# Seven stores for two batch tiles instead of eight, the fifth across the end of a tile

## The chip, the cores and the metric

The kernel runs on one core of one Trainium2 chip. The metric is the time on the device in microseconds (us), the median of several executions. A ratio between two kernels is the mean time of one kernel's runs over that of the other's runs of the same rounds, so it isn't quite the ratio of the medians that are quoted.

## The reference

For every batch row and every pair of fields i < j of 32 fields with 64 values each, the vector of field i goes through the pair's own 64 x 64 matrix, and the result is multiplied element by element with the vector of field j.

```python
vi = inputs[:, i_idx, :]              # (4096, 496, 64), pairs i < j
vj = inputs[:, j_idx, :]
vdotw = jnp.einsum('bpd,pde->bpe', vi, W)
inter = vdotw * vj
return inter.reshape(B, -1)           # (4096, 31744) float32
```

520 MB are written, 42 MB are read. There are 32 batch tiles of 128 rows.

## The kernel before

TensorE multiplies into PSUM, VectorE (DVE) multiplies PSUM by the fields and writes into a ring in SBUF, and SyncE issues the stores from the ring to memory. "Unit" below means 64 columns: 64 float32 numbers, 256 B, in each of 128 rows. The work goes by two neighbouring fields at a time: step p (0 to 15) of a tile, "the pair of fields p" below, makes all products of the fields 2p and 2p + 1 with the later ones. That is 61 - 4p units, a tile 496. The ring has 440 units. A store is issued when all of its units are made, and a store that doesn't fit behind the last one begins again at 0. A product that writes to a place of the ring must wait until every earlier store from that place has landed.

```python
STORES = [[0, 1], [2, 3], [4, 5, 6], [7, 8, 9, 10, 11, 12, 13, 14, 15]]
RING = 28160
# ...
for t in range(NT):
    xt = slot[t]
    # ... input loads, two tiles each, from the ACT queue
    for s, group in enumerate(STORES):
        if at + store_w[s] > RING:
            at = 0
        osb = ring[:, at : at + store_w[s]]
        at += store_w[s]
        o0 = off[2 * group[0]]
        for p in group:
            # ... transposes of the input, matmuls into PSUM,
            #     DVE products into osb
        nc.sync.dma_start(
            out=out[:, t * cols + o0 : t * cols + o0 + store_w[s]], in_=osb
        )
```

Of the kernel before, what the change touches and what calls it, by code (L numbers as in the profile page):

```python
# [1 line left out]

# [6 lines left out]

F32 = mybir.dt.float32  # L10
ALU = mybir.AluOpType

P = 128
BANK = 512
BANKS = 8

STORES = [[0, 1], [2, 3], [4, 5, 6], [7, 8, 9, 10, 11, 12, 13, 14, 15]]

LOADS = [[0], [1], [2, 3], [4, 5, 6], [7, 8, 9, 10, 11, 12, 13, 14, 15]]


FIRST_HALF_AT, SECOND_HALF_AT = 9, 3
RING = 28160


def x_slots(NT):


    loads = [[(0, 0)]]
    for t in range(1, NT, 2):  # L30
        if t + 1 == NT:
            loads.append([(t, 1)])
        elif loads[-1][-1] == (t - 1, 2):
            loads.append([(t + 1, 0), (t, 1)])
        else:
            loads.append([(t, 1), (t + 1, 2)])
    return loads


@with_exitstack  # L40
def pair_bilinear_kernel(
    ctx: ExitStack,
    tc: tile.TileContext,
    x: bass.AP,
    w: bass.AP,
    out: bass.AP,
    F: int,
    D: int,
):
























    nc = tc.nc
    NT = out.shape[1] * 2 // (F * (F - 1) * D)
    NPR = F // 2

    width = [(F - 1 - i) * D for i in range(F)]
    off = [sum(width[:i]) for i in range(F)]
    cols = sum(width)  # L80


    woff = [i % 2 * D + sum(width[i % 2 : i : 2]) for i in range(F)]
    store_w = [sum(width[2 * p] + width[2 * p + 1] for p in g) for g in STORES]

    const = ctx.enter_context(tc.tile_pool(name="const", bufs=1))
    psum = ctx.enter_context(tc.tile_pool(name="ps", bufs=1, space=bass.MemoryType.PSUM))

    ident = const.tile([P, P], F32, tag="ident", name="ident")
    make_identity(nc, ident)  # L90

    def runs(tl, a, b, n):

        ap = tl[:, a : a + n]
        return bass.AP(ap.tensor, ap.offset, [list(ap.ap[0]), [b - a, 2], list(ap.ap[1])])

    xbuf = const.tile([P, 3 * F * D], F32, tag="x", name="x")
    x_loads = x_slots(NT)
    slot = {t: xbuf[:, ts(s, F * D)] for load in x_loads for t, s in load}

    def load_x(load):

        at = sum(len(before) for before in x_loads[: x_loads.index(load)]) * P * F * D
        n = len(load) * F * D
        s = load[0][1]
        nc.scalar.dma_start(
            out=xbuf[:, s * F * D : s * F * D + n],
            in_=x[at : at + P * n].rearrange("(p c) -> p c", p=P),
        )

    pring = psum.tile([P, BANKS * BANK], F32, tag="pring", name="pring")
    bank = 0

    def take_banks(n):

        nonlocal bank
        if bank + n > BANKS:
            bank = 0
        got = pring[:, bank * BANK : (bank + n) * BANK]
        bank = (bank + n) % BANKS  # L120
        return got

    xT = const.tile([P, NPR * P], F32, tag="xT", name="xT")

    def transpose_x(xt, g):

        n = 2 * BANK // P
        pt = take_banks(2)
        for c in range(n):
            nc.tensor.transpose(pt[:, ts(c, P)], xt[:, ts(n * g + c, P)], ident)  # L130
        nc.scalar.copy(xT[:, ts(g, 2 * BANK)], pt)  # L131

    ring = const.tile([P, RING], F32, tag="ring", name="ring")
    at = 0

    load_x(x_loads[0])
    w_sb = const.tile([P, sum(width[0::2])], F32, tag="w", name="w")
    done = 0
    for g in LOADS:

        upto = woff[2 * g[-1]] + width[2 * g[-1]]
        nc.sync.dma_start(out=w_sb[:, done:upto], in_=w[:, done:upto])
        done = upto

    transpose_x(slot[0], 0)
    for t in range(NT):
        xt = slot[t]
        for load in x_loads:
            if min(load)[0] == t + 1:
                load_x(load)  # L150
        for s, group in enumerate(STORES):
            if at + store_w[s] > RING:
                at = 0
            osb = ring[:, at : at + store_w[s]]
            at += store_w[s]
            o0 = off[2 * group[0]]
            for p in group:
                if p == SECOND_HALF_AT:
                    transpose_x(xt, 1)
                if p == FIRST_HALF_AT and t + 1 < NT:  # L160
                    transpose_x(slot[t + 1], 0)
                first = (width[2 * p] - 1) % BANK + 1
                for c1 in range(first, width[2 * p] + 1, BANK):
                    n = first if c1 == first else BANK
                    c0 = c1 - n
                    odd = width[2 * p + 1] and c1 > D
                    pm = take_banks(2)
                    for h in range(1 + bool(odd)):
                        a = woff[2 * p + h] + c0 - h * D
                        nc.tensor.matmul(  # L170
                            pm[:, h * BANK : h * BANK + n],
                            xT[h * D : (h + 1) * D, ts(p, P)],
                            w_sb[h * D : (h + 1) * D, a : a + n],
                            start=True,
                            stop=True,
                        )
                    xj = xt[:, (2 * p + 1) * D + c0 : (2 * p + 1) * D + c1]
                    o = [off[2 * p + h] - o0 + c0 - h * D for h in range(2)]
                    if odd and (c0 or c1 < width[2 * p]):
                        nc.vector.tensor_tensor(  # L180
                            runs(osb, o[0], o[1], n),
                            runs(pm, 0, BANK, n),
                            bass.AP(xj.tensor, xj.offset, [xj.ap[0], [0, 2], xj.ap[1]]),
                            ALU.mult,
                        )
                    else:
                        for h in range(1 + bool(odd)):
                            nc.vector.tensor_tensor(  # L188
                                osb[:, o[h] + h * D : o[h] + n],
                                pm[:, h * (BANK + D) : h * BANK + n],  # L190
                                xj[:, h * D :],
                                ALU.mult,
                            )
            nc.sync.dma_start(
                out=out[:, t * cols + o0 : t * cols + o0 + store_w[s]], in_=osb
            )


# [30 lines left out]
```

## Time and profile before

| | before |
|---|---|
| median | 1336.87 us (6 runs, 1336.71 to 1337.26) |
| DMA engines | 98.9% of the span, 422 GB/s |
| DVE | 1183.4 us busy, 89% |
| stores | 128, of 118, 102, 123, 153 units a tile |

The prediction below reckons from 1337.05 us, one of these six runs.

How to read it: the share of the DMA queues says that sixteen DMA engines work nearly all the time, so the kernel ends when the bytes are moved. One row of the groups by shape is kept here (its columns: busy us, mean ns of one, then the idle time before):

```profile
L180 DVE TENSOR_TENSOR ring<-pring,x 128x1024 f32<-128x1024 f32 x768 | 902.7, 1217 | 16.6 <-PE pring L170 4.2 <-DMA out_dram<-ring 1.5
```

### The profile page before, as it was taken

The page shows a single profiled execution, that of the slowest core. Times are in us where ns is not written, and L with a number is a line of the kernel's source. Part 1 is how long each engine was busy: PE and PEld are TensorE (multiplying, and loading weights), DVE is VectorE, ACT ScalarE, POOL GpSimd, SP SyncE. Part 2 cuts the span into 40 slices and gives each one's busy share as a digit, 9 for nine tenths or more (in the row PEclk, how much of TensorE's full clock was granted, in tenths as well). Part 3 has the DMA queues.
Part 4 walks back from the last instruction along what each step waited for, and adds up shares of the span by engine and source line. Part 5 has one row for each costly group of instructions (what it writes and reads, how often), then busy time and mean ns, then how long its engine had stood idle before and what let it go on. Part 6 is the DMA issues. An engine that isn't in the chain of part 4 may idle for free.

```text
span 1335.1 us, 13080 instructions
## 1 busy us (share of the span) xinstructions
PE 1160.6 (87%) x5376; PEld 544.9 (41%) x5376; DVE 1183.4 (89%) x1376; ACT 66.1 (5%) x65; POOL 0.7 (0%) x6
## 2 busy tenths in 40 slices
PE   6998989989899898998989889798998979989893
PEld 3443334443344443444444444344443434354441
DVE  5998989989899898998989899898998989989894
ACT  0000000000000000000000000000000000000000
POOL 0000000000000000000000000000000000000000
PEclk9999999989899999998989999899999999989997
DMA  9999999999999999999999999999999999999998
GB/s 397 433 430 430 431 428 430 418 433 430 413 425 410 436 414 427 426 414 433 405 432 431 419 429 411 432 426 421 428 413 430 426 407 417 429 421 423 429 425 352
DMA packets 21659, 562.87 MB, mean 422 GB/s; under 512 B 2400, under 2 KB 2400, under 8 KB 2656
## 3 DMA queue, kind: packets, MB, share of 16 engines
q1 hardware_dynamic: 19152, 528.49, 92.8%
q10 hardware_dynamic: 2448, 33.56, 5.9%
q8 instruction: 42, 0.69, 0.2%
q14 instruction: 17, 0.14, 0.0%
HBM read 41.94 MB, written 520.09 MB: 421 GB/s over the span
## 4 chain that ended last, share of the span: by engine, by line
DMA 47%; DVE 38%; issue 9%; PE 5%; DVEq 0%; ACT 0%
DMA out_dram<-ring 46%; DVE ring L180 32%; DVE ring L188 5%; PE pring L170 5%; DMA x<-in_x_dram 1%; DVEq L180 0%; PE pring L130 0%; ACT xT L131 0%; DVEq L225 0%; DVEq L188 0%
## 5 line engine op out<-in xcount | busy, mean ns | idle before, releaser
L170 PE MATMUL pring<-w,xT 64*128 64x512 f32 (+4 forms) x4864 | 1098.4, 564 | 146.4 <-DVE ring L180 133.5
L180 DVE TENSOR_TENSOR ring<-pring,x 128x1024 f32<-128x1024 f32 (+3 forms) x1056 | 1104.1, 1108 | 131.4 <-DMA out_dram<-ring 102.6
L170 PEld LDWEIGHTS pring<-w,xT 64*128 64x128 f32 x4864 | 489.3, 191 | 711.7 <-DVE ring L180 533.0
L131 ACT COPY xT<-pring 128x1024 f32<-128x1024 f32 x64 | 64.8, 1012 | 1224.1 <-PE pring L130 1224.1
L188 DVE TENSOR_TENSOR ring<-pring,x 128x64 f32<-128x64 f32 (+3 forms) x320 | 97.7, 356 | 2.6 <-DMA out_dram<-ring 1.9
L130 PEld LDWEIGHTS pring<-ident,x 128*128 128x128 f32 x512 | 55.6, 142 | 58.8 <-DVE ring L180 50.2
L130 PE MATMUL pring<-ident,x 128*128 128x128 f32 x512 | 70.8, 282 | 8.6 <-DMA x<-in_x_dram 8.6
L131 ACT ACT_TABLE_LOAD x1 | 1.3, 1283 | 1.7 <-PEq L221 1.7
masks.py:199 POOL TENSOR_SCALAR_AFFINE_SELECT ident<-ident 128x128 f32<-128x128 f32 x1 | 0.3, 292 | 0.1
masks.py:197 POOL MEMSET ident<- 128x128 f32 x1 | 0.2, 204 | 0.3 <-POOLq L221 0.3
L221 POOL MEMSET const-bfloat16-1.0<- 128x1 bf16 x1 | 0.1, 101 | 0.0
L221 POOL MEMSET const-uint8-127<- 128x1 uint8 x1 | 0.1, 101 | 0.0
L221 POOL MEMSET const-float32-0.0<- 128x1 f32 x1 | 0.1, 98 | 0.2 <-issue 0.2
L221 POOL MEMSET const-float32-1.0<- 128x1 f32 x1 | 0.1, 98 | 0.0
## 6 DMA issues: line engine op xcount, KB each, us to landing
out_dram<-ring SPq DMA_DIRECT2D x32, 4896.0 KB, 17.7
out_dram<-ring SPq DMA_DIRECT2D x32, 3936.0 KB, 18.1
out_dram<-ring SPq DMA_DIRECT2D x32, 3776.0 KB, 18.3
out_dram<-ring SPq DMA_DIRECT2D x32, 3264.0 KB, 18.6
x<-in_x_dram ACTq DMA_DIRECT2D x15, 2048.0 KB, 20.4
w<-in_w_dram SPq DMA_DIRECT2D x1, 2592.0 KB, 28.1
x<-in_x_dram ACTq DMA_DIRECT2D x2, 1024.0 KB, 12.8
w<-in_w_dram SPq DMA_DIRECT2D x1, 2016.0 KB, 22.2
```

The lines of the kernel that those rows point to most:

```text
L130: nc.tensor.transpose(pt[:, ts(c, P)], xt[:, ts(n * g + c, P)], ident)
L131: nc.scalar.copy(xT[:, ts(g, 2 * BANK)], pt)
L170: nc.tensor.matmul(pm[:, h * BANK : h * BANK + n], xT[h * D : (h + 1) * D, ts(p, P)], w_sb[h * D : (h + 1) * D, a : a + n], start=True, st ...
L180: nc.vector.tensor_tensor(runs(osb, o[0], o[1], n), runs(pm, 0, BANK, n), bass.AP(xj.tensor, xj.offset, [xj.ap[0], [0, 2], xj.ap[1]]), ALU ...
L188: nc.vector.tensor_tensor(osb[:, o[h] + h * D : o[h] + n], pm[:, h * (BANK + D) : h * BANK + n], xj[:, h * D :], ALU.mult,)
L221: nc = bacc.Bacc("TRN2", target_bir_lowering=False, num_devices=1)
```

## The change

The intent: fewer and larger stores, and cuts that fill the ring better. The stores are now counted over two tiles; the fifth takes the last three pairs of fields of one tile and the first three of the next.

```diff
-STORES = [[0, 1], [2, 3], [4, 5, 6], [7, 8, 9, 10, 11, 12, 13, 14, 15]]
+STORES = [0, 2, 5, 9, 13, 19, 23]
...
+    pair_at = [u // NPR * cols + off[u % NPR * 2] for u in range(NT * NPR)] + [NT * cols]
+    starts = [2 * NPR * k + u for k in range(NT // 2) for u in STORES] + [NT * NPR]
...
-        for s, group in enumerate(STORES):
-            if at + store_w[s] > RING:
-                at = 0
-            osb = ring[:, at : at + store_w[s]]
-            at += store_w[s]
...
+        for p in range(NPR):
+            u = t * NPR + p
+            if u in starts:
+                o0 = pair_at[u]
+                end = starts[starts.index(u) + 1]
+                size = pair_at[end] - o0
+                if at + size > RING:
+                    at = 0
+                osb = ring[:, at : at + size]
+                at += size
...                       # matmuls and products as before
-            nc.sync.dma_start(
-                out=out[:, t * cols + o0 : t * cols + o0 + store_w[s]], in_=osb
-            )
+            if u + 1 == end:
+                nc.sync.dma_start(out=out[:, o0 : o0 + size], in_=osb)
```

The stores are then of 118, 147, 140, 76, 186, 172 and 153 units.

## The prediction

> **What bounds the kernel now.** I read the page from the busy line to the slices, the DMA queues and the chain of waits; then the waits by engine, the groups by shape, and the chain in order of time for two tiles in mid-run.
>
> The page, with the median of 1337.05 us beside it:
>
> ```profile
> PE 1160.6 (87%) x5376; PEld 544.9 (41%) x5376; DVE 1183.4 (89%) x1376; ACT 66.1 (5%) x65; POOL 0.7 (0%) x6
> DMA  9999999999999999999999999999999999999998
> ...
> q1 hardware_dynamic: 19152, 528.49, 92.8%
> q10 hardware_dynamic: 2448, 33.56, 5.9%
> q8 instruction: 42, 0.69, 0.2%
> ...
> DMA 47%; DVE 38%; issue 9%; PE 5%; DVEq 0%; ACT 0%
> ```
>
> The queues' shares add to 98.9% of sixteen engines' span: the DMA engines are the bound, VectorE comes second at 89%. The chain alternates between DMA and DVE because each wait for ring space is followed by the work that fills the next store. That reading makes DVE look like half of the bound; it isn't, as long as the DMA queue never empties while DVE works.
>
> Who waits for a store's landing, and how seldom:
>
> ```profile
> DVE ring L180 <- DMA out_dram<-ring: 102.6, 44, 6.2
> DVE ring L180 <- PE pring L170: 17.9, 9, 13.5
> ```
>
> The figures are us in total, times and the longest. DVE stands 103 us, 2.3 us at a time, for ring space; PE costs it almost nothing after the start.
>
> The chain in order of time, between two stores of the last nine pairs of a tile:
>
> ```profile
> 582.09 21.96 DMA out_dram<-ring
> 604.05 0.03 issue
> 604.10 0.04 issue
> 604.14 1.15 DVE ring L180 x2
> ...
> 625.43 17.16 DMA out_dram<-ring
> 642.59 0.03 issue
> ```
>
> The store of 153 field widths (unit below: one width of 64 columns, 256 B a row) is issued at 582.09 and landed at 604.05, and DVE resumes 0.09 us later. Its packets themselves take 8 x 1.451 = 11.6 us on each of sixteen engines (trace: 39168 B rows, median 1451 ns, eight rows an engine), so about 4.7 us of the 17.16 were older work in the queue, 0.45 were the gap between the last packet and the last completion mark; the 21.96 also holds an input load (16384 B rows, 8 x 0.611 = 4.9 us).
>
> **One engine is late.** In the trace each store leaves sixteen completion marks. In mid-run fifteen come within about 1.5 us, and the last one 3.7 to 4.7 us behind most of them; the run's last packets end at 1329.9 to 1331.2 us on fifteen engines and at 1333.7 on one. When a 153 store is issued most engines have just run dry (first packet 0.83 us after issue; 27 such gaps, 12 us of mean engine time altogether), but the late engine still has 4.1 to 5.5 us queued. So before, the late engine never idles after the start, and the gaps of the others cost nothing. Its pace: two tiles take 81.9 us (mean of the issues from 91.19 to 1237.94, 14 pairs of tiles), less 4.9 for the input load, over 992 units: 77.6 ns a unit. The other engines need 8 x 1119 ns / 118 = 75.9.
>
> DVE's own pace, start to start without waits, added per store from the trace: pairs 0-1 8.5 us, 2-3 7.4, 4-6 9.1, 7-15 12.2; 37.1 us a tile of 496 units, or 75 ns a unit, against 41 us of DMA a tile. DVE is 10% faster than the late engine with its input load, but hardly 4% faster than its stores alone.
>
> **What the Trainium skill says.** (1) "DMA: Bandwidth & Descriptors", "Why a DMA increments its semaphore by 16 and not by 1": engines finish independently and only the full count means that all data landed. The trace agrees: sixteen marks a store, and DVE goes by the last. (2) The same page, "Specifications", gives about 27 GiB/s an engine and a 435 GB/s ceiling. The trace has 26.98 to 27.01 GB/s an engine for all four row sizes, 432 for sixteen: stores are at the ceiling, so larger ones can't be faster. (3) Same page, "Rules for kernel authors": at least 1 MiB a DMA, and coalesce small ones. All stores already have 3264 to 4896 KB, so this rule promises nothing here. (4) "Runtime: NRT & Kernel Launch", "Instruction fetch mechanics": instructions come by DMA in 16 KiB blocks of 256. The trace has 42 packets of 16384 B on the instruction queue, and 10752 PE instructions are 42 x 256. That such packets make one engine late is likely; no view proves it, and they don't change.
>
> **The change part by part.** Arithmetic, matmuls, DVE operations (1376) and their order stay. Only where a store begins and ends, and where it lies in the ring, changes. Units of the stores: before 118, 102, 123, 153 each tile; after 118, 147, 140, 76, 186, 172, 153 for two tiles.
>
> Removed: 16 stores of 128. On an engine each costs a completion mark (9 ns) and eight packet starts; from 968 ns at 26112 B and 1451 ns at 39168 B the start costs about 2 ns. 16 x (9 + 8 x 2) ns = 0.4 us. SyncE issues (0.33 us each) are off the path. So -0.4.
>
> Moved, ring: 28160 columns are 440 units, a store that doesn't fit starts again at 0. Before, the passes use 343, 373, 394, 378 units (mean 372); after 405, 434, 418, 402, 325 (mean 397). This is the gain the change is after: more data in flight at most places. But it is a gain only where it lets the late engine work, and that one has no gap to give back.
>
> Moved, granularity: nothing of a store can leave until all of it is made. 186 units are 13.7 us of DVE and 172 are 12.6, against 12.2 for the largest before. Worse, the small store of 76 sits just before 186, so the queue must live through 13.7 us on what is left plus 76 units.
>
> I follow the late engine's queue through the weak place, which recurs every four tiles: ring positions 153 at 172, 118 at 0, 147 at 118, 140 at 265, 76 at 0, 186 at 76. The 147 store crosses position 172, so it waits in its second pair of fields for the landing of the 153 store. At that moment only 118 units are queued: 118 x 77.6 = 9.2 us, less 0.5 passed between the last packet and DVE's start: 8.6.
> - DVE ends the 147 store: three operations of 1.13 and a pair of 3.3, with the restart 6.8 us. Queue left 1.8; the store adds 147 x 77.6 = 11.4.
> - 140 units: DVE 10.4. Left 13.2 - 10.4 = 2.8; adds 10.9.
> - 76 units: DVE 6.1. Left 13.7 - 6.1 = 7.5; adds 5.9.
> - 186 units: DVE 13.7. Left 13.4 - 13.7 = -0.3. With 0.83 us from issue to first packet the late engine stands 1.1 us.
> No ring wait falls in these four steps: the places they write were left by stores that landed earlier. The other passes, counted the same way, keep at least 2 us. The weak place occurs at stores 19, 33, 47 and so on by 14, seven times in 112 (in the first pass the ring is empty and nothing has fallen behind). 7 x 1.1 = 8 us.
>
> Start and end: weights fill the DMA engines until about 30 us, while the first stores are ready at 23 and 34; no loss. The last store is 153 units as before, so the tail is the same.
>
> Sum: 1337.05 - 0.4 + 8 = 1344.5; I take 1344.
>
> **The rivals.**
> (a) The fuller ring ends the gaps before the 153 stores. If mean engine time bounded the kernel, at most the 12 us of gaps came back: 1325. For it: 27 gaps at the same place of the tile, and the chain's waits. Against it: the late engine has 4.1 us or more left at each of them, and ends 2.5 us or more behind the others.
> (b) The queue never quite empties, because DVE is 1 to 2% quicker there than I added. Then the late engine works through and the time is 1336.6: unchanged. For it: the shortfall at the weak place is only 0.3 us plus the start latency.
> (c) DVE is slower there: a restart after a wait, or a transpose in the 186 store, costs another 0.5 to 1 us, and other weak places (the 147 store keeps 1.8 us) run dry as well: 1350 or somewhat above. Each us lost in the four-tile cycle costs 7 to 8 us in all, which is why the size is less sure than the sign.
>
> **Range and chances.** The floor is the late engine's own work, about 1336, since the change takes no bytes away; the upper side is an idle of 2 us a cycle. Time 1344, range 1335.5 to 1351. Faster by 2% (below 1310) would need the bytes to move quicker than the engines' 27 GB/s: 0.01. Slower by 2% (above 1363.8) needs nearly 4 us idle a cycle: 0.02. Within 2%: 0.97.
>
> **What would show it.** Right: the DVE operations keep their durations; DVE waits in total stay near 100 to 120 us but in fewer, longer pieces; the DMA row shows dips every four tiles (about 164 us), and at the 186 store in ring position 76 first packets come on all sixteen engines only after its issue; packets on the store queue fall by 16 x 144 = 2304. Wrong: a last completion mark that is still over 4 us away at every issue (then b), or one that comes with the others, so that gaps do count (then a); or new PE waits in the DVE list.

## The result, and the profile after

The changed kernel takes 1346.57 us (median of 6 runs, 1345.93 to 1347.53), before 1336.87; the ratio is 1.0073, with a 95% interval of 1.006 to 1.0086. That is slower by 9.7 us, and by the 2% mark the same.

From the page of the changed kernel:

```profile
span 1344.8 us, 13029 instructions
PE 1180.8 (88%) x5376; PEld 551.9 (41%) x5376; DVE 1182.4 (88%) x1376; ACT 66.1 (5%) x65; POOL 0.7 (0%) x6
DMA  9999999999999999999999999999999999999999
...
q1 hardware_dynamic: 16848, 528.49, 92.0%
...
DMA 41%; DVE 33%; PE 18%; issue 7%; DVEq 0%; ACT 0%
```

The bytes are the same, the packets fewer by 2304, as worked out ahead. Note how little the row of digits tells: it is all nines, although the stores' packets stop on all engines seven times. A slice is 33.6 us, and a pause of 2 us disappears in it. The chain shows PE at 18% where it had 5%. That is no new bound: DVE's waits for PE grew from 17.9 to 22.9 us only. The ring waits now fall inside a store, and behind them DVE takes the products as PE brings them.

The waits of DVE by engine (us in total, times, longest), and the row of its largest shape:

```profile
DVE ring L187 <- DMA out_dram<-ring: 113.9, 39, 5.7
DVE ring L187 <- PE pring L177: 22.9, 20, 13.6
```

```profile
L187 DVE TENSOR_TENSOR ring<-pring,x 128x1024 f32<-128x1024 f32 x768 | 903.0, 1217 | 57.4 <-DMA out_dram<-ring 38.7 <-PE pring L177 8.3
```

A product still takes 1217 ns. DVE waits 11 us more for the ring, in fewer pieces, at other shapes.

Now the place that the prediction names. SyncE's part of the timeline, from 712 to 730 us (start, us, what, how many), says that two stores are issued in this stretch, at 713.50 (76 units) and, 13.7 us later, at 727.20 (186 units):

```profile
713.50 14.03 SPq L202 DMA_DIRECT2D out_dram<-ring  x2
```

DVE in the same stretch works without a pause (two earlier lines are left out):

```profile
714.71 12.46 DVE L187 TENSOR_TENSOR ring<-pring,x 128x896 f32<-128x896 f32 x12
727.08 0.21 DVE L195 TENSOR_TENSOR ring<-pring,x 128x64 f32<-128x64 f32 x1
727.27 3.49 DVE L187 TENSOR_TENSOR ring<-pring,x 128x1024 f32<-128x1024 f32 x3
```

And three stretches around it, with the busy time of each engine, the granted clock, the DMA share and GB/s:

```profile
722.00:725.30 3.30, 3.29 (x18) 1.46 (x16) 3.30 (x5) 0.00 (x0) 0.00 (x0) 1.00 0.91 382
725.30:728.10 2.80, 2.58 (x12) 1.09 (x12) 2.80 (x4) 1.01 (x1) 0.00 (x0) 1.00 0.49 205
728.10:731.00 2.90, 2.90 (x16) 1.35 (x14) 2.90 (x4) 0.00 (x0) 0.00 (x0) 1.00 0.84 361
```

The view counts a packet, with all its bytes and all its time, where it starts, so the 0.49 of the middle stretch holds packets that began at 728.02 and ran on after it. Cut at the ends of the stretch, the engines were busy for 0.17 of it, and for all of the stretches on both sides. Packet by packet, most engines have nothing from 725.4 on, the last one ends its share of the 76 store at 727.38, and the first packet of the 186 store comes at 728.02, 0.83 us after the issue. For 0.65 us no engine moves anything. I call this a dry-out. The trace of the changed kernel has seven, at 232, 397, 562, 727, 893, 1058 and 1224 us, 165 us apart, which is four tiles. They are 0.65 to 0.86 us long, the last one 0.17, 4.6 us together. In the last one a single packet of an instruction fetch (0.92 us) runs; the stores' queue is empty for 1.09 us there, and for 5.5 us in all seven. The kernel before has none after its loads.

"The last engine" below is the one of the sixteen whose queue lasts longest at that moment; it isn't always the same one. Its queue at the issue of each store, worked out ahead and read from the packets of three of these places (last packet of the store before, less the time of the issue):

| store | worked out | near 397 | near 562 | near 727 |
|---|---|---|---|---|
| 147 | 1.8 us | 1.71 | 1.77 | 1.72 |
| 140 | 2.8 | 2.62 | 3.56 | 2.39 |
| 76 | 7.5 | 7.90 | 8.00 | 7.08 |
| 186 | -0.3 | -0.03 | 0.07 | 0.18 |

### The profile page after: what moved, and what is told of

Its sections match the earlier page's. It is cut to its first block, busy times and chain, and to the rows that moved or that the text cites. A ratio compares the mean times of both kernels' runs of the same rounds, so it can differ in the third digit from the quotient of the medians.

```text
span 1344.8 us, 13029 instructions
## 1 busy us (share of the span) xinstructions
PE 1180.8 (88%) x5376; PEld 551.9 (41%) x5376; DVE 1182.4 (88%) x1376; ACT 66.1 (5%) x65; POOL 0.7 (0%) x6
## 4 chain that ended last, share of the span: by engine, by line
DMA 41%; DVE 33%; PE 18%; issue 7%; DVEq 0%; ACT 0%
DMA out_dram<-ring 40%; DVE ring L187 29%; PE pring L177 17%; DVE ring L195 4%; PE pring L134 1%; DMA x<-in_x_dram 1%; DVEq L187 0%; ACT xT L135 0%; DVEq L231 0%
## 5 line engine op out<-in xcount | busy, mean ns | idle before, releaser
L177 PE MATMUL pring<-w,xT 64*128 64x512 f32 (+4 forms) x4864 | 1118.7, 573 | 138.9 <-DVE ring L187 127.7
L187 DVE TENSOR_TENSOR ring<-pring,x 128x1024 f32<-128x1024 f32 (+3 forms) x1056 | 1103.0, 1108 | 147.3 <-DMA out_dram<-ring 113.9
L177 PEld LDWEIGHTS pring<-w,xT 64*128 64x128 f32 x4864 | 496.4, 195 | 719.9 <-DVE ring L187 533.0
```

The costliest lines, as they stand in the source:

```text
L177: nc.tensor.matmul(pm[:, h * BANK : h * BANK + n], xT[h * D : (h + 1) * D, ts(p, P)], w_sb[h * D : (h + 1) * D, a : a + n], start=True, st ...
L187: nc.vector.tensor_tensor(runs(osb, o[0], o[1], n), runs(pm, 0, BANK, n), bass.AP(xj.tensor, xj.offset, [xj.ap[0], [0, 2], xj.ap[1]]), ALU ...
```

## The experiments

Theory 1 is the one of the prediction: the loss is made at one place in four tiles, where DVE needs longer for the 186 store than the queue lasts. The rivals are that the ring positions cost it (A), that only a part of it is due to the dry-outs and the rest to slower transfers (B), that fewer and larger stores are worse as such (C), that DVE isn't on the path there (D), or that DVE is the bound everywhere (E). Eleven kernels ran. All were correct.

| run | median us | over before | dry-outs | no engine moving, us |
|---|---|---|---|---|
| changed kernel | 1346.57 | 1.0073 | 7 | 4.6 |
| e1_split186 | 1337.26 | 1.0003 | 0 | 0 |
| e2_tile_end | 1336.19 | 1.0000 | 0 | 0 |
| e3_cut_at_18 | 1387.03 | 1.0376 | 15 | 39.8 |
| e4_ring_443 | 1353.58 | 1.0125 | 9 | 8.0 |
| e8_split_443 | 1337.16 | 1.0003 | 0 | 0 |
| e9_late_dve_weak | 1355.46 | 1.0140 | 7 | 12.8 |
| e10_late_dve_strong | 1345.91 | 1.0068 | 6 | 4.4 |
| e11_late_dve_before | 1337.07 | 1.0001 | 0 | 0 |

The last two columns are counted from the packets of each profile, after the loads of the start and up to the last store. The changed kernel wasn't run again with the others; where they are compared with it, both stand against the kernel before, which took 1336.77 to 1337.03 us in all rounds.

### The store of 186 units cut in two

```diff
-STORES = [0, 2, 5, 9, 13, 19, 23]
+STORES = [0, 2, 5, 9, 13, 17, 19, 23]
```

> The changed kernel with the 186-unit store cut in two after its first 76 units (76 + 110); every byte keeps its ring position, so all ring waits stay possible as they were. Theory 1 (the queue runs dry before the 186 store, and that is the whole loss): the queue of the late engine then never falls below about 1 us at an issue, no stretch without any packet on any engine, 1336 to 1338 us, 0.993 of the changed kernel. Rival A (the new ring positions and their waits cost the time, whatever the size of the store): stays at 1345 to 1347. Rival B (only the 4.6 us in which all engines stood are due to it, the other 5 us are slower transfers of the long rows): 1341 to 1342.

Measured: 1337.26 us (1337.10 to 1337.38, 5 runs), 1.0003 of before. No dry-out is left; the last engine never has less than 1.6 us queued at an issue. The same time in this kernel, with a store of 110 issued at 723.44:

```profile
722.00:725.30 3.30, 3.08 (x16) 1.20 (x16) 3.30 (x5) 0.85 (x1) 0.00 (x0) 1.00 0.94 401
725.30:728.10 2.80, 2.80 (x18) 1.40 (x16) 2.80 (x4) 0.00 (x0) 0.00 (x0) 1.00 1.09 464
728.10:731.00 2.90, 2.81 (x16) 0.94 (x12) 2.90 (x4) 0.00 (x0) 0.00 (x0) 1.00 1.05 450
```

(A share above 1 comes from the same way of counting: cut at the ends, all three stretches are full.) The whole 9.3 us come back, by a cut that moves no byte in the ring. Rivals A and B fall: the ring positions by themselves don't cost the time, and all of the loss hangs on the moment when the first 76 of these 186 units are let go. The cut is made in all sixteen stores of 186, not only at the seven weak places; that the place matters is shown by the tied products below.

### The cut at the end of the tile

```diff
-STORES = [0, 2, 5, 9, 13, 19, 23]
+STORES = [0, 2, 5, 9, 16, 19, 23]
```

> Still seven stores for two tiles and nearly the same ring, but the boundary moves from pair 13 to the end of the tile: 118, 147, 140, 91, 171, 172, 153 units; no store crosses a tile. Theory 1: the store in the weak place is ready 1.1 us of work earlier behind a longer one before it, so the late engine has about 1 us left at its issue, just over the 0.83 us start: 1336 to 1338, the 0.4 us of the 16 saved stores unseen. Rival C (fewer and larger stores are worse as such): 1344 or more. Rival B: 1341 to 1342.

Measured: 1336.19 us (1336.01 to 1339.06, 5 runs), ratio to before 1.0000. At the issues of the 171 store in the weak place 1.0 to 1.3 us are left, as worked out, where 0.83 are needed. So seven stores for two tiles are no worse than eight: rival C falls. Nor are they better.

### More of the same: a store of 225 units

```diff
-STORES = [0, 2, 5, 9, 13, 19, 23]
+STORES = [0, 2, 5, 9, 13, 18, 23]
```

> The reverse dose: the boundary after 186 moves one pair forward, 118, 147, 140, 76, 133, 225, 153 units. By the same arithmetic of the queue 225 units need 16.4 us of DVE on a queue of 2.5 to 3 plus 133 x 0.0776 = 10.3 us, short by 3 us, with the start latency 4 us of idle on the late engine at each, now every two tiles (15 times): theory 1 gives 1337 + 58 = 1395, between 1388 and 1405. Rival C would see the mean store unchanged and give about 1347. If each dry-out costs another 0.7 us beyond the idle time, as the changed kernel's 9.7 us against 4.6 us of full idle would have it, 1405.

Measured: 1387.03 us (1386.28 to 1388.21), 1.0376. That is 50 us over before, a little below the range that was given (1388 to 1405), and five times the changed kernel's loss for one boundary moved by one pair of fields. The page now does show it in its slices:

```profile
DMA  9999899998999989999899998999989999899998
GB/s 396 435 405 427 357 423 436 383 433 377 404 433 382 433 374 412 403 417 424 370 419 412 409 433 351 431 412 407 430 354 436 400 409 434 347 436 400 418 419 358
```

There are fifteen dry-outs, as worked out, but they alternate between 3.5 to 4.6 and 0.8 to 1.9 us (the last is 2.7); all had been put at 4. Why every second one is short was not followed.

### The changed kernel with a slightly larger ring

```diff
-RING = 28160
+RING = 28352
```

> The changed kernel's stores with a ring of 28352 columns (443 units) instead of 28160 (440): now 325 + 118 units fit in one pass, and all later positions shift. Sizes are as in the changed kernel. Theory 1: the 186 store now follows a wait for ring space that ends later, the late engine keeps about 1.4 us at its issue and 0.5 us at one 153 store in four tiles: 0.3 us idle at each of 7 places, 1338 to 1341. Rival C (store sizes): 1345 to 1347 as before.

Measured: 1353.58 us, 1.0125: three more units of ring make the kernel 7 us slower. Theory 1 had the direction of the change wrong here, 1338 to 1341. The packets show two reasons. Between 397 and 760 us, the 186 store at position 0 comes when 0.17 to 0.5 us are left where 1.4 had been worked out, and the 153 store when 0.02 to 0.7 are left where it was 0.5, so both can run dry. DVE's times were as reckoned in this stretch; the queue drained faster. Between the landings of this stretch the last engine needed 75.7 ns a unit (11.13 us for 147, 10.59 for 140), not the 77.6 that I had taken from the mean pace. The mean pace of the last engine holds over many tiles, not over the 30 us between a wait and the next weak place. A margin of 1 us in this arithmetic can't be trusted.

The two longest pauses, 2.2 us at 1090 and 2.1 at 1258, come later, and are more than half of the 8.0. There DVE was slower. Inside the 153 store it waited twice for PE (the time in brackets):

```profile
1083.48 0.82 DVE L187 TENSOR_TENSOR ring<-pring,x 128x640 f32<-128x640 f32 x1 [0.86 <-PE pring L177]
1084.93 3.05 DVE L187 TENSOR_TENSOR ring<-pring,x 128x1024 f32<-128x1024 f32 x3 [0.62 <-PE pring L177]
```

From the end of the ring wait to the issue DVE took 13.8 us, where it had taken 12.4 before the issue at 427, and the queue was empty 1.4 us before the store came. The granted TensorE clock was 0.76 in this stretch and in the one before 1258; it was 0.86 to 1.00 at the four earlier issues of this store at 427, 594, 759 and 924, where DVE didn't wait for PE inside the store. That the slower clock made these two pauses long is what the trace suggests; no run tests it.

### The split kernel with the larger ring

```diff
-RING = 28160
+RING = 28352
-STORES = [0, 2, 5, 9, 13, 19, 23]
+STORES = [0, 2, 5, 9, 13, 17, 19, 23]
```

> The split kernel (eight stores, 186 cut in 76 and 110) with the ring of 443 units: by the arithmetic of the queue the late engine keeps over 5 us at every issue, though the ring of 443 alone made the changed kernel slower. Theory 1: no dry-out, and no gain over the kernel before either, since its late engine already works without a pause: 1336 to 1338. Rival F (the ring of 443 itself is bad, for another reason than the queue): 1344 or more. Were a fuller queue worth something by itself, below 1334.

Measured: 1337.16 us (1337.06 to 1337.32), 1.0003. The ring of 443 units isn't bad in itself (rival F), and a deeper queue brings nothing: the last engine keeps 4.6 us or more at every issue, and before took 1336.77 in these rounds.

### Three tests that failed: DVE work that went elsewhere

To put DVE on trial directly, three products into a scratch tile were added in one tile of four, at the weak place, at a strong place, and in the kernel before:

```diff
...                       # the scratch tile "waste"
+            if p == 14 and t % 4 == 0:          # t % 4 == 2 in the second
+                for _ in range(3):
+                    nc.vector.tensor_tensor(waste, xt[:, 0:320], xt[:, 320:640], ALU.mult)
```

> The changed kernel with three more DVE products (128x320, into a scratch tile, 0.48 us each by the row of that shape, so 1.2 to 1.45 us together) inside the 186 store of every tile 0, 4, 8...: that is the weak place of the queue, seven times, and once in the first pass where the queue is full. 9.8 to 11.5 us of DVE work in all. Theory 1: at the weak place the queue is empty when the store comes, so all of it shows: 7 x 1.3 = 9 us, 1354 to 1357. Rival D (DVE isn't on the path, the loss is in the transfers): unchanged, 1346 to 1347.

> The same three DVE products in the 186 store of tiles 2, 6, 10..., eight times as well: there the queue still holds over 4 us of the late engine at the issue. Theory 1: the work disappears in DVE's waits for ring space, 1346 to 1348. If DVE work costs wherever it lies (rival E, DVE as the bound), as in the run before: 1354 to 1357.

> The kernel before with the same three products at the same pair of tiles 0, 4, 8..., inside its 153 store, which is its own tightest place: the late engine keeps 4.1 to 5.5 us there. Theory 1: 2.8 us or more are left, nothing shows, 1336.5 to 1338. Rival E: 1346.

Measured: 1431.42, 1412.04 and 1399.56 us, some 63 us or more over what each was made from, where 0 or 9 were expected. From the waits of the first:

```profile
DVE waste L204 <- DMA x<-in_x_dram: 121.7, 8, 17.5
```

The products need nothing but an input tile, and they were put far ahead in DVE's order: in the first run they started at 8.7 us, and later always within the making of a 118 store instead of the 186. DVE stood 12 to 15 us each time, in the mean, for an input load. These runs say nothing on the question. They show that an added instruction measures the place where it ends up, and that its place has to be tied by its data.

### The same with tied products

Four products of 128x192 read what DVE has just written to the ring:

```diff
...                       # the scratch tile "waste"
+            if p == 14 and t % 4 == 0:          # t % 4 == 2 in the second; p == 12 and xj[:, 0:192] in the kernel before
+                for _ in range(4):
+                    nc.vector.tensor_tensor(waste, osb[:, o[0] : o[0] + 192], xj, ALU.mult)
```

> The three runs with scratch products on the input tile failed as tests: the products had no producer on DVE, were ordered far ahead, and DVE stood some 15 us each time for an input load (100 to 122 us in all). Now four products 128x192 take what DVE has just written to the ring, so they stay inside the 186 store of the changed kernel, in tiles 0, 4, 8...; 0.27 to 0.35 us each, 1.1 to 1.4 us a time. Theory 1: the queue is empty there, seven times the whole of it shows: 8 to 10 us over the changed kernel, 1354 to 1357. Rival D (DVE is not on the path there): 1346 to 1347.

> The same four products in the 186 store of tiles 2, 6, 10..., where the last engine had 4.3 to 4.4 us queued at the issue: theory 1 leaves 3 us, so 1346 to 1348.5 as the changed kernel. Rival E (DVE time costs wherever it lies): 1354 to 1357.

> The kernel before with the same four products inside its 153 store of tiles 0, 4, 8...: the last engine had 4.1 to 5.5 us queued there, about 3 are left. Theory 1: 1336.5 to 1338. Rival E: 1345 to 1348.

In all three the products lie where they were meant to, at 346 or 347 ns each, 1.38 us a time. From the first (duration minimum, median, maximum; first and last start):

```profile
L204 DVE TENSOR_TENSOR waste<-ring,x x32: 345/346/359, 51.0 to 1220.8; 128x192 f32<-128x192 f32 x32
```

Measured: at the weak place 1355.46 us, 8.9 over the changed kernel, for 7 x 1.38 = 9.7 us of work that was expected to show. The pauses grew from between 0.65 and 0.86 us to between 1.9 and 2.2 at six places, and to 0.8 at the seventh. At the strong place 1345.91, nothing. In the kernel before 1337.07, nothing (1.0001). The same 11 us of DVE work cost 9 us or none, by where they lie. Rivals D and E fall, and theory 1 stands in all three.

## Why the prediction was right

The prediction was 1344 us, between 1335.5 and 1351, and within 2%; measured were 1346.57. By its steps:

- **The bound.** DMA, with an engine that never idles before. Right as far as the runs go: the products added to the kernel before cost nothing, and neither a deeper queue nor fewer stores gave anything (1337.16 and 1336.19).
- **The saved stores.** 0.4 us were put down, and none can be seen: the kernel with the cut at the tile's end has as few stores as the changed one, and its ratio to before is 1.0000 with an interval of 0.9986 to 1.0013. That is too wide to tell 0.4 us from nothing.
- **The fuller ring gains nothing (rival a).** Right. e1 has the ring of the changed kernel without its dry-outs and takes the time of before. (The prediction counted 27 gaps before the 153 stores; by the packets 29 of these 32 stores start 0.83 us after their issue.)
- **The weak place.** Right in position, period, number and in the queue at each of its four stores (the table above). This is the step that carries the result, and the split store shows it to be the cause.
- **The size of it.** 1.1 us at seven places was the term, 7.7 us in sum. The pauses in which nothing moved were 0.65 to 0.86 us at six places and 0.17 at the seventh, 4.6 in sum, so this term was put too high (5.5, if the stores' queue alone is counted). The loss was still larger, 9.7: a dry-out cost more than its pause. Beyond the pause it took 5.1 us for 7 dry-outs here, 10.4 for 15 in e3 (50.2 less 39.8), 8.8 for 9 in e4 (16.8 less 8.0) and 5.6 for 7 in e9 (18.4 over before less 12.8): 0.7 to 1.0 us each. This was not in the sum at all. So the sum came within 3 us partly by luck: one term was 3 us too high, another of 5 was missing.
- **What this rest is.** The trace suggests it; no run tests it. One engine's packets run some 20 to 50 ns longer than the others' in both kernels. In the kernel before it lies last, with over 1 us to the next. An engine that fetches instructions loses about 0.4 us at each fetch and lies 2 to 3 us ahead of it in mid-run, so the fetches cost nothing there. A dry-out lets all engines start again together. At the next one, the engine with the long packets was done 0.35 to 1.3 us before the last; at 727 the last one was the engine that had just fetched (a packet longer by 410 ns, three microseconds before). So the engine with the most work to do waits not only through the pause but already before it. At the four dry-outs where it can be followed (397, 893, 1058, 1224) it stood 1.2, 2.1, 1.2 and 1.6 us; an estimate from their mean for seven is 10.8 us, near the 9.7 lost.
- **Which engine is late.** I called it likely that the instruction fetches make the late engine late. The same packets speak against it for the kernel before: from 270 us on, the engine hit by a fetch mostly ends 2 us or more before the last, where it could be followed.
- **The waits.** 100 to 120 us were forecast, 113.9 came, in 39 pieces where it had been 44. The longest didn't grow, though: 5.7 against 6.2. New waits for PE, named as a sign against the forecast, did come: 20 instead of 9, 22.9 us instead of 17.9. They lie elsewhere: from the issue of the 76 store to that of the 186 store DVE is busy all the time at each of the seven weak places, 13.6 to 13.7 us long. The split kernel has 6 such waits, of 17.1 us.
- **The signs.** At the weak place the first packets came on all engines only after the issue, as said. The dips forecast for the DMA row didn't show: it is all nines.
- **The engines' pace.** The prediction sets the 27 GiB/s an engine of the Trainium skill ("DMA: Bandwidth & Descriptors", "Specifications") beside 27 GB/s in the trace. 27 GiB/s would be 29 GB/s; it is the ceiling of 435 GB/s that the trace's 432 agrees with.

The range's upper side, and rival (c) in it, was the more useful half: each further microsecond at the weak place did cost 7 to 8, as e9 shows.

## What to carry to other kernels

When the DMA queue bounds a kernel and stores are made from a ring, the size of a store is a latency: follow the queue from each wait for space to the next issues, and look for a small store ahead of a large one. Cutting the store at which the queue runs out gave back everything here, while a slightly larger ring made it worse, since it shifts all later waits. A margin worked out by such arithmetic isn't safe within about a microsecond of the start latency: 1.4 us worked out were 0.17 to 0.5 in e4, though about 1 us held in e2. Pauses under 1 us didn't show in shares or slices: look for stretches without any packet, and cut the packets at the ends of a stretch before reading its share.

## What the Trainium skill lacked or had wrong

- "DMA: Bandwidth & Descriptors", "Rules for kernel authors", tells to coalesce small transfers and gives no upper side. "Perfetto Trace Analysis", "DMA Optimizations", does say that splitting lets some start sooner, but for engines that are generally idle; here they were busy for 98% of the span. One store of 186 units (5952 KB) instead of two, of 76 and 110, cost 9.3 us of 1337, and one of 225 units 50 us, because none of it can leave before all of it is made.
- "DMA: Bandwidth & Descriptors" says that engines finish independently, not how far apart they drift in a long stream: in mid-run of the kernel before, the last of the sixteen completion marks of a store (each engine leaves one when its share is done) came 3.5 us or more behind half of the others, while a store's own packets take 7.7 to 11.6 us.
- The same page, "Latency and other measured facts", gives some 600 ns to the first byte of a transfer from these queues. From the start of the issue to the first packet of an idle engine it was 0.83 us in every dry-out, or 0.50 from the end of the issue, which takes 0.33; the page doesn't say from where it counts.
- "Runtime: NRT & Kernel Launch", "Instruction fetch mechanics", calls the crossing of a 16 KiB block mostly hidden. The fetches share the DMA engines with the stores: a packet of a store that met one took about 0.4 us longer (378 to 412 ns in most of the 42 cases of the kernel before).
- No page, as far as I looked, says that a dry-out costs more than its pause: 0.7 to 1.0 us more each, in four kernels.
